# Two gated feed-forwards of layer 2 moved into the last steps of the rotary attention's loop, with silu written by tanh

## The chip, the core and the metric

The kernel runs as one program on one core of a Trainium2 chip. The metric is device time in microseconds for one execution of the whole program, the median of several executions. A profile of one further execution gives the trace that is read below. Engines are named as in the profile: PE is TensorE (matrix multiply), PEld its weight loads, DVE is VectorE, ACT is ScalarE, POOL is GpSimd, SP issues most DMAs.

## What is computed

Four layers act on one residual `x` of shape 4 x 1024 x 128 (batch, sequence, channels), all float32. Every layer is a "macaron": half a feed-forward, an attention, half a feed-forward, each behind a layer norm without gain. The reference, cut to the end of layer 1 and the start of layer 2 as the kernel numbers its stages (the reference calls the first of these modules L1):

```python
def _L1_ffn_ref(x, w_gate, w_up, w_down):        # DIM 128, HIDDEN 384, weights int / 127
    gate = jnp.einsum('bsd,hd->bsh', x, wg)
    up = jnp.einsum('bsd,hd->bsh', x, wu)
    h = jax.nn.silu(gate) * up
    return jnp.einsum('bsh,dh->bsd', h, wd)
...
x = x + 0.5 * _L1_ffn_ref(_layernorm(x, axis=-1), L1_ffn_w_gate, L1_ffn_w_up, L1_ffn_w_down)
x = x + _L1_attn_ref(_layernorm(x, axis=-1), L1_attn_w_qkv, L1_attn_w_out, L1_attn_b_out)
x = x + 0.5 * _L1_ffn_ref(_layernorm(x, axis=-1), L1_ffn_w_gate, L1_ffn_w_up, L1_ffn_w_down)
x = x + 0.5 * _L2_ffn_ref(_layernorm(x, axis=-1), L2_ffn_router_w, ...)    # mixture of experts, top 2 of 8
x = x + _L2_attn_ref(...)                                                   # linear attention with decay
```

`_L1_attn_ref` is a rotary softmax attention with 16 heads of 8 channels over 1024 positions. The third line, the gated feed-forward after the attention, is what the change is about: it stands between the rotary attention and the experts of the next layer, and each of the four batches has one of its own.

## The kernel before

**Stages.** `run` (L1284) goes through four stages in order: `l0`, `l1_attn`, `l2`, `l3`. The residual lies in SBUF for the whole run, one tile `X[b]` of 128 channels x 1024 positions for each batch. The stage `l1_attn` is the rotary attention. The stage `l2` begins with the gated feed-forward that follows it in the reference and then does the experts and the linear attention.

**The rotary attention, `l1_attn` (L629).** The work is cut into 256 units: 4 batches x 4 groups of four heads x 16 units, each unit one 128-wide slice against 512 positions. One loop (L800 to L826) with step `k` runs a pipeline. In step `k`, for each of two pairs of heads, it issues
- `greatest` (L713): two matmuls with 32 rows each into a PSUM tile `two` (128 x 1024, two banks), and a maximum over it on DVE (L720);
- `scores` (L735): two matmuls with 32 rows into PSUM tiles `s`, and the exponentials `e` on ACT (L743), for the unit `k - 11`;
- `values` (L745): matmuls of `e` with the values into the PSUM tile `o`, for the unit before that one.

Between steps, generators in the list `running` are advanced by one `yield` each (L826). They are the background steps: `shifted` (L722), `normalized` (L754), and `prepare` (L662), which for the next batch does the layer norm (project with the centring matrix `cen`, square it on ACT, sum it by eight 128 x 1 matmuls `var`, a square root on ACT, spread it by eight matmuls `bc`, and scale it on DVE to `xn`) and the projections with their rotation. `prepare` is started at `k % 64 == 10` for the next batch, so it runs three times inside the loop and not at all for the last 64 steps. From `k = 256` on there is no `greatest`, since only the second and third part of the pipeline are left; the loop ends with `k = 267`, and a last loop (L827) drains `running`.

**Order.** PE's order in this stage is the order of the program (`manual_schedule`, L641). The tiles `two` come from a pool with two buffers (L638), the tiles `s` from one with three, `o` has one; together they are all eight banks of PSUM. Every background step that uses PE takes one of the two `two` buffers and holds it until its last reader is done. The other engines are ordered by the scheduler of the framework, and each runs its own queue in order.

**Layer 2, `layer2` (L1255) and `l1_ffn` (L588).** `lanes` (L1188) interleaves generators by the costs that they yield. `first0` to `first3` are the gated feed-forwards of the batches (`l1_ffn`): layer norm of a batch, then in each half of 512 positions three pairs of matmuls `wg` and `wu` (128 x 128 with 128 x 512), `Silu` on ACT (L613), the product on DVE (L616), three matmuls `wd`, and `add_half` (L246), which adds half the result to `X`. `first0` and `first2` lie in one lane and `first1` and `first3` in another, so 0 and 1 run first. `route` for batches 0 and 1 (L276) waits for `first0` and `first1`; it computes the gating and the lists of tokens by which `experts` (L424) gathers its rows. No expert starts before a route is done.

Of the kernel before, what the change touches and what calls it, by code (L numbers as in the profile page):

```python
# [12 lines left out]
AF = mybir.ActivationFunctionType  # L13
ALU = mybir.AluOpType
AX = mybir.AxisListType

P = 128
# [4 lines left out]
HALF = 512  # L22
# [6 lines left out]
HIDC = 3  # L29
# [176 lines left out]
class Macaron:  # L206
# [36 lines left out]
            parts[part] = v  # L243
        return parts

    def add_half(self, b, c, o):  # L246

        X = self.X[b]
        self.nc.vector.scalar_tensor_tensor(X[:, c], o, 0.5, X[:, c], ALU.mult, ALU.add)

# [225 lines left out]
    def combine(self, ps, wp, batches, b, plan):  # L476

        nc = self.nc
        gt = len(batches) * NT
        n = batches.index(b)  # L480
        if n == 0:
            yield 9
        y = []
        for c in range(2):
            y.append(self.t(wp, [P, NT, D], f"c_y{c}", bufs=1))
            r = slice(c * gt * P + n * S, c * gt * P + (n + 1) * S)
            nc.sync.dma_start(out=y[c], in_=plan["res"][r, :].rearrange("(i p) d -> p i d", p=P))
        for h in range(2):
            tp = self.t(ps, [P, 4, P], "bank")
            for j in range(4):  # L490
                i = 4 * h + j
                nc.scalar.mul(y[0][:, i, :], y[0][:, i, :], plan["p1"][:, n * NT + i, :])
                nc.vector.scalar_tensor_tensor(
                    y[1][:, i, :], y[1][:, i, :], plan["p2"][:, n * NT + i, :], y[0][:, i, :], ALU.mult, ALU.add
                )
                nc.tensor.transpose(tp[:, j, :], y[1][:, i, :], self.c0["ident"])
            self.add_half(b, slice(h * HALF, (h + 1) * HALF), tp.rearrange("p i t -> p (i t)"))
        yield 6


# [87 lines left out]
    def l1_ffn(self, ps, wp, m, b):  # L588
        nc, c0 = self.nc, self.c0
        X = self.X[b]  # L590
        bank = lambda shape=(P, HALF): self.t(ps, list(shape), "bank")
        halves = [slice(h * HALF, (h + 1) * HALF) for h in range(2)]
        sq, xc = self.t(wp, [P, S], "sq", bufs=1), self.t(wp, [P, S], "xc", bufs=1)
        for c in halves:
            cen = bank()
            self.mm(cen, c0["center"], X[:, c])
            nc.scalar.activation(sq[:, c], cen, AF.Square)
            nc.vector.tensor_copy(xc[:, c], cen)
        r = self.scales(ps, wp, sq, "f")
        yield 4  # L600
        for hf, c in enumerate(halves):
            bc = bank((P, 4, P))
            for j in range(4):
                i = 4 * hf + j
                self.mm(bc[:, j, :], r[:, i : i + 1].to_broadcast([P, P]), c0["ident"])
            xn = self.t(wp, [P, HALF], "xn")
            nc.vector.tensor_tensor(xn, xc[:, c], bc.rearrange("p i t -> p (i t)"), ALU.mult)
            h = self.t(wp, [P, HIDC, HALF], "h", bufs=1)
            for i in range(HIDC):
                g = bank()  # L610
                self.mm(g, m["wg"][:, i, :], xn)
# [9 lines left out]
            self.add_half(b, c, o)  # L621
            yield 3


# [1 line left out]

    def l1_attn(self, m, c1):  # L629
        nc = self.nc  # L630
        scale = HD ** -0.5
        LEAD, RING = 11, 4
        v = nc.vector
        PE = mybir.EngineType.PE
        with ExitStack() as ctx:
# [23 lines left out]
                    self.mm(o[:, h * HALF : (h + 1) * HALF], w, x[:, h * HALF : (h + 1) * HALF])  # L659
                return o  # L660

            def prepare(b):  # L662
                c, X = self.c0, self.X[b]
                cen = project(c["center"], X)
                sq = self.t(self.lnp, [P, S], "sq", bufs=1)
# [15 lines left out]
                    self.mm(bc[:, i * P : (i + 1) * P], r[:, i : i + 1].to_broadcast([P, P]), c["ident"])  # L681
                xn = self.t(self.lnp, [P, S], "xn")
                v.tensor_tensor(xn, xc, bc, ALU.mult)
                yield
                yield
                for w, wt, tag in ((m["wq"], m["wqt"], "qd"), (m["wk"], m["wkt"], "kd")):
                    t1 = self.t(wp, [P, S], "rot1", bufs=1)
                    v.tensor_tensor(t1, c1["cos"], project(w, xn), ALU.mult)
                    yield
                    t2 = self.t(wp, [P, S], "rot2", bufs=1)  # L690
                    v.tensor_tensor(t2, c1["sin"], project(wt, xn), ALU.mult)
                    out = dense[b, tag] = self.t(wp, [P, S], tag, bufs=1)
                    nc.gpsimd.tensor_tensor(out, t1, t2, ALU.add)
                    yield
# [59 lines left out]
            def normalized(chunk, o):  # L754
# [20 lines left out]
                if g4 == 3:  # L775
# [15 lines left out]
                    v.scalar_tensor_tensor(X[:, c], y, m["bo"], X[:, c], ALU.add, ALU.add)  # L791
                    yield

            for _ in prepare(0):
                pass
            for n in range(RING):
                spread(n)
            units = B * 4 * 16
            running, nms, qms, pending, o = [], {}, {}, None, None
            for k in range(units + LEAD + 1):  # L800
# [3 lines left out]
                    spread(k // 16 + RING - 1)  # L804
                if k % 64 == 10 and k // 64 + 1 < B:
                    running.append(prepare(k // 64 + 1))
                if first is not None and first % 8 == 0:
                    nms[first // 8] = self.t(wp, [P, 4, 2, 4], "nm", bufs=3)
                    qms[first // 8] = self.t(wp, [P, HALF], "qm", bufs=3)
# [378 lines left out]
    def lanes(self, *lanes):  # L1188
        lanes = [list(lane) for lane in lanes]
        clock, active, done = [0.0] * len(lanes), [None] * len(lanes), set()  # L1190
        while any(lanes) or any(active):
            ready = []
            for n, lane in enumerate(lanes):
                if active[n] is None and lane and done.issuperset(lane[0][1]):
                    name, _, start = lane.pop(0)
                    active[n] = (name, start())
# [58 lines left out]
    def layer2(self, moe, m, right, enter, ffn):  # L1255
# [11 lines left out]
            yield 0  # L1267

        def more(route):
            first = lambda b: (f"first{b}", (), ffn(pf[b % 2], (side, main)[b % 2] if b < 2 else side, b))  # L1270
            attn = lambda b: (f"middle{b}", (f"combine0{b}", "swap"), lambda: self.l2_attn(side, pa[b % 2], m, decay, b))
            return (
                [first(0), first(2), attn(0), attn(2)],
# [9 lines left out]

    def run(self, stages):  # L1284
        nc = self.nc
        self.X = []
        self.c0 = self.load("c0")
        for b in range(B):
            X = self.t(self.res, [P, S], f"x{b}")
# [20 lines left out]
        for n, name in enumerate(stages):  # L1310
# [61 lines left out]
```

## Time and profile before

| what | value |
|---|---|
| runs | 3285.68, 3293.57, 3298.78 us (median 3293.57) |
| the profiled execution | 3296.3 us, span of its profile 3294.4 us |
| busy: PE / PEld | 2875.3 us (87%) / 1685.8 us (51%) |
| busy: DVE / ACT / POOL | 1826.5 us (55%) / 1649.2 us (50%) / 807.0 us (24%) |
| last `values` matmul of the rotary attention ends | 2035.13 us |
| first matmul of batch 2's feed-forward starts | 2081.07 us |
| first matmul with an expert's weights starts | 2159.66 us |
| mean granted clock of PE | 0.905 |

The page of the profile has six parts; the second shows the span in 40 slices of 82.4 us, with each engine's busy share in tenths. The rotary attention fills slices 11 to 24, layer 2 begins in slice 24. A timeline lists instructions by start and duration, with the idle time before them in brackets and what ended it. A table by stretches gives each engine's busy time between two times, and PE's granted clock there. A matmul in float32 shows as two records of PE.

### The profile page before, as it was taken

The page shows a single profiled execution, that of the slowest core. Times are in us where ns is not written, and L with a number is a line of the kernel's source. Part 1 is how long each engine was busy: PE and PEld are TensorE (multiplying, and loading weights), DVE is VectorE, ACT ScalarE, POOL GpSimd, SP SyncE. Part 2 cuts the span into 40 slices and gives each one's busy share as a digit, 9 for nine tenths or more (in the row PEclk, how much of TensorE's full clock was granted, in tenths as well). Part 3 has the DMA queues.
Part 4 walks back from the last instruction along what each step waited for, and adds up shares of the span by engine and source line. Part 5 has one row for each costly group of instructions (what it writes and reads, how often), then busy time and mean ns, then how long its engine had stood idle before and what let it go on. Part 6 is the DMA issues. An engine that isn't in the chain of part 4 may idle for free.

```text
span 3294.4 us, 48535 instructions
## 1 busy us (share of the span) xinstructions
PE 2875.3 (87%) x18206; PEld 1685.8 (51%) x18206; DVE 1826.5 (55%) x3160; ACT 1649.2 (50%) x3640; POOL 807.0 (24%) x748
## 2 busy tenths in 40 slices
PE   6888637878879999999999999988988977899997
PEld 6766426766643333333333333586777865344333
DVE  3376877774226676676776772431555521355664
ACT  3565524658613565566566565444444534444442
POOL 2565405552340000000000000046434454011110
PEclk7989858889977999999999999979989988788997
DMA  4766414663500000000000000157565666000000
GB/s 151 227 186 188 140 42 130 185 188 115 168 9 7 4 6 4 6 6 4 21 5 6 1 1 9 42 152 245 171 185 147 199 197 194 0 0 0 7 7 13
DMA packets 122890, 277.64 MB, mean 84 GB/s; under 512 B 18016, under 2 KB 67296, under 8 KB 122528
## 3 DMA queue, kind: packets, MB, share of 16 engines
q1 hardware_dynamic: 101792, 231.77, 23.8%
q0 software_dynamic: 20864, 42.77, 4.3%
q8 instruction: 144, 2.36, 0.3%
q14 instruction: 90, 0.74, 0.1%
HBM read 238.43 MB, written 31.85 MB: 82 GB/s over the span
## 4 chain that ended last, share of the span: by engine, by line
PE 74%; DVE 12%; ACT 5%; issue 4%; DMA 3%; POOL 1%; another core or an unknown queue 0%; SPq 0%; ACTq 0%; DVEq 0%; POOLq 0%
PE bank L227 40%; PE two L227 17%; PE o L227 8%; PE s L227 4%; DVE nm L720 2%; ACT e_h L468 2%; PE wave L1010 1%; DVE prod L545 1%; PE bank L461 1%; DMA c_y<-res 1%; DVE sc L530 1%; ACT L468 1%; DMA e_w<-in_l0m_dram 1%; DVE prod L528 1%; DVE e_x L463 1%
## 5 line engine op out<-in xcount | busy, mean ns | idle before, releaser
L720 DVE TENSOR_REDUCE nm<-two 128x2 f32<-128x1024 f32 x512 | 626.9, 1225 | 288.3 <-PE s L227 268.9
L743 ACT ACTIVATE e<-s 128x512 f32<-128x512 f32 x1024 | 556.4, 595 | 405.6 <-PE s L227 402.6
L468 ACT ACTIVATE e_h<-bank,e_w 128x128 f32<-128x128 f32 x1304 | 454.8, 368 | 511.6 <-PE bank L227 388.4
L227 PE MATMUL bank<-e_x,e_w 128*128 128x128 f32 x2608 | 569.3, 318 | 154.5 <-ACT e_h L468 79.9
L227 PE MATMUL s<-qm,kz 32*128 32x512 f32 x2048 | 634.1, 643 | 0.8 <-ACT e L743 0.8
L227 PE MATMUL two<-kz,qz 32*128 32x512 f32 x2048 | 593.2, 664 | 21.3 <-DVE nm L720 2.5
L227 PEld LDWEIGHTS bank<-e_x,e_w 128*128 128x128 f32 x2608 | 413.9, 204 | 291.3 <-ACT e_h L468 144.4
L457 POOL DMA_INDIRECT e_xg<-rows,g_source x326 | 334.4, 1026 | 835.1 <-DVE g_target L412 354.2
L227 PE MATMUL bank<-e_w,e_h 128*128 128x128 f32 x2608 | 445.7, 291 | 12.3 <-ACT e_h L468 6.9
L442 POOL DMA_INDIRECT res<-e_y,g_target x326 | 373.5, 1146 | 337.0 <-DVE e_y L441 152.7
L227 PEld LDWEIGHTS bank<-e_w,e_h 128*128 128x128 f32 x2608 | 378.8, 205 | 23.0 <-ACT e_h L468 13.3
L227 PE MATMUL o<-e,va 128*32 128x256 f32 x4096 | 328.8, 392 | 0.1
L441 DVE TENSOR_TENSOR e_y<-bank,e_w 128x128 f32<-128x128 f32 x326 | 94.3, 290 | 403.7 <-PE bank L227 317.0
L227 PEld LDWEIGHTS two<-kz,qz 32*128 32x128 f32 x2048 | 159.7, 189 | 239.9 <-issue 164.0
L227 PEld LDWEIGHTS o<-e,va 128*32 128x32 f32 x4096 | 81.0, 108 | 390.3 <-issue 370.3
L227 PEld LDWEIGHTS s<-qm,kz 32*128 32x128 f32 x2048 | 206.9, 183 | 10.9 <-issue 7.7
L708 POOL COPY va<-vd 128x256 f32<-128x256 f32 x16 | 6.7, 433 | 626.3 <-PE o L227 538.0
L1115 POOL TENSOR_TENSOR z<-st,r 128x512 f32<-128x512 f32 x32 | 46.2, 1445 | 417.1 <-DVE st L1108 333.7
L463 DVE COPY e_x<-bank 128x128 f32<-128x128 f32 x326 | 93.0, 285 | 92.2 <-PE bank L461 67.6
L227 PE MATMUL bank<-g_cols,g_lanes 128*128 128x39 f32 (+1 forms) x512 | 90.5, 341 | 28.9 <-DVE g_cols L392 28.8
L461 PE MATMUL bank<-c,e_xg 128*128 128x128 f32 x326 | 95.0, 291 | 21.7 <-DMA e_xg<-rows,g_source 21.6
L227 PEld LDWEIGHTS bank<-g_cols,g_lanes 128*128 128x128 f32 x512 | 91.2, 270 | 32.5 <-issue 31.4
(300 smaller groups left out, 3694.0 us busy)
## 6 DMA issues: line engine op xcount, KB each, us to landing
e_w<-in_l0m_dram SPq DMA_DIRECT2D x170, 578.0 KB
e_w<-in_l2m_dram SPq DMA_DIRECT2D x156, 578.0 KB
c_y<-res SPq DMA_DIRECT2D x32, 512.0 KB
rows<-g_xt SPq DMA_DIRECT2D x16, 512.0 KB
e_xg<-rows,g_source POOLq DMA_INDIRECT x326
res<-e_y,g_target POOLq DMA_INDIRECT x326
x<-in_x_dram SPq DMA_DIRECT2D x4, 512.0 KB
qz<-qd SPq DMA_DIRECT2D x64, 32.0 KB
```

Source lines behind the costliest of these rows:

```text
L227: self.nc.tensor.matmul(out, lhsT, rhs, start=start, stop=stop)
L441: nc.vector.tensor_tensor(y, o, w[:, MOE_W - D :], ALU.add)
L442: ins = nc.gpsimd.indirect_dma_start(out=res[:, :], out_offset=at(target[:, k : k + 1]), in_=y, in_offset=None)
L457: nc.gpsimd.indirect_dma_start(out=xg, out_offset=None, in_=rows[:, :], in_offset=at(source[:, k : k + 1]))
L461: nc.tensor.transpose(tp, xg, self.c0["ident"])
L463: nc.vector.tensor_copy(x, tp)
L468: nc.scalar.activation(h[:, fc, :], up[:, fc, :], func, bias=w[:, 2 * FC * P + fc : 2 * FC * P + fc + 1])
L528: v.tensor_tensor(pr, q.unsqueeze(2).to_broadcast(sh), k.unsqueeze(1).to_broadcast(sh), ALU.mult)
L530: v.tensor_reduce(sc, pr, AX.X, ALU.add)
L720: v.tensor_reduce(nm[:, it, h, 2 * pair : 2 * pair + 2], s, AX.X, ALU.max, negate=True)
L743: nc.scalar.activation(es[g], s, AF.Exp, scale=scale)
L1115: (pool if i else v).tensor_tensor(z, st[:, 0:HALF], r, ALU.mult)
```

## The change

`prepare` is split: its layer norm becomes `normal(b, out)`, which `prepare` calls and the new `feed` calls too. `feed(b, w)` does the gated feed-forward of batch `b` as background steps: the six yields of the layer norm, then for each half three steps with `wg` and `wu` into one `two` tile, an empty step, and one step with the three `wd` matmuls into a `two` tile and the addition to `X`. `feeds()` does this for batches 0 and 1 one after the other, and is put into `running` at `k = 240`, when both batches have left the attention. Its 32 steps reach beyond the loop's end at `k = 267`, so the last four run in the drain. `AF.Silu` is replaced by `tanh(gate / 2)` on ACT, `(tanh + 1) * gate` and the product with `up` on DVE, and a factor 0.25 in place of 0.5. The intermediate tiles use the buffers `rot1` and `rot2` of the last rotation. In `layer2`, `first0` and `first1` become empty tasks that are done at once. The feed-forwards of batches 2 and 3 stay where they are, with `Silu`.

```diff
+    def add_part(self, b, c, o, part=0.5):
-        self.nc.vector.scalar_tensor_tensor(X[:, c], o, 0.5, X[:, c], ALU.mult, ALU.add)
+        self.nc.vector.scalar_tensor_tensor(X[:, c], o, part, X[:, c], ALU.mult, ALU.add)
...
-            def prepare(b):
+            def normal(b, out):
                 c, X = self.c0, self.X[b]
                 cen = project(c["center"], X)
...
+                out.append(xn)
                 yield
                 yield
+
+            def prepare(b):
+                held = []
+                yield from normal(b, held)
+                (xn,) = held
...
+            def feed(b, w):
+                held = []
+                yield from normal(b, held)
+                (xn,) = held
+                for hf in range(2):
+                    c = slice(hf * HALF, (hf + 1) * HALF)
+                    h01, h2 = (self.t(wp, [P, 2, HALF], tag, bufs=1) for tag in ("rot1", "rot2"))
+                    hs, act = [h01[:, 0], h01[:, 1], h2[:, 0]], h2[:, 1]
+                    for i in range(HIDC):
+                        gu = two((P, 2, HALF))
+                        self.mm(gu[:, 0], w["wg"][:, i, :], xn[:, c])
+                        self.mm(gu[:, 1], w["wu"][:, i, :], xn[:, c])
+                        nc.scalar.activation(act, gu[:, 0], AF.Tanh, scale=0.5)
+                        v.scalar_tensor_tensor(act, act, 1.0, gu[:, 0], ALU.add, ALU.mult)
+                        v.tensor_tensor(hs[i], act, gu[:, 1], ALU.mult)
+                        yield
+                    yield
+                    o = two((P, HALF))
+                    for i in range(HIDC):
+                        self.mm(o, w["wd"][:, i, :], hs[i], start=i == 0, stop=i == HIDC - 1)
+                    self.add_part(b, c, o, 0.25)
+                    yield
+
+            def feeds():
+                for b in fed:
+                    yield from feed(b, fed[b])
...
+                if k == units - 16:
+                    running.append(feeds())
...
-            first = lambda b: (f"first{b}", (), ffn(pf[b % 2], (side, main)[b % 2] if b < 2 else side, b))
+            first = lambda b: (f"first{b}", (), ffn(pf[b % 2], (side, main)[b % 2] if b < 2 else side, b) if b not in self.fed else tuple)
...
-                    self.l1_attn(weights("l1a"), weights("c1"))
+                    self.fed = {b: weights("l1f") for b in range(2)} if "l2" in stages else {}
+                    self.l1_attn(weights("l1a"), weights("c1"), self.fed)
```

More of the change, by code (lines that the diff above doesn't have):

```diff
@@ L244, in load @@
         return parts
-    def add_half(self, b, c, o):
+    def add_part(self, b, c, o, part=0.5):
         X = self.X[b]
-        self.nc.vector.scalar_tensor_tensor(X[:, c], o, 0.5, X[:, c], ALU.mult, ALU.add)
+        self.nc.vector.scalar_tensor_tensor(X[:, c], o, part, X[:, c], ALU.mult, ALU.add)
     def centered(self, w, n):
@@ L496, in combine @@
                 nc.tensor.transpose(tp[:, j, :], y[1][:, i, :], self.c0["ident"])
-            self.add_half(b, slice(h * HALF, (h + 1) * HALF), tp.rearrange("p i t -> p (i t)"))
+            self.add_part(b, slice(h * HALF, (h + 1) * HALF), tp.rearrange("p i t -> p (i t)"))
         yield 6
@@ L620, in l1_ffn, with l1_attn @@
                 self.mm(o, m["wd"][:, i, :], h[:, i, :], start=i == 0, stop=i == HIDC - 1)
-            self.add_half(b, c, o)
+            self.add_part(b, c, o)
             yield 3
-    def l1_attn(self, m, c1):
+    def l1_attn(self, m, c1, fed):
         nc = self.nc
@@ L1195, in lanes @@
                     name, _, start = lane.pop(0)
-                    active[n] = (name, start())
+                    active[n] = (name, iter(start()))
                     clock[n] = max(clock[n], min([clock[o] for o in range(len(lanes)) if o != n and active[o]] or [0]))
@@ L1285, in run @@
         nc = self.nc
-        self.X = []
+        self.X, self.fed = [], {}
         self.c0 = self.load("c0")
```

## Prediction, made before the changed kernel ran

> **What bounds the kernel now.** I read the slices of the page first, then a table by stretches around the change, then timelines inside them.
>
> ```profile
> PE   6888637878879999999999999988988977899997
> PEclk7989858889977999999999999979989988788997
> ```
>
> Slices 11 to 24 are the rotary attention and the start of layer 2. PE is at nine tenths or more throughout, with its clock whole except for short stretches.
>
> ```profile
> 1935.12:1993.60 58.48, 57.95 (x525) 20.05 (x524) 41.69 (x40) 35.72 (x66) 0.00 (x0) 1.00 0.00 1
> 1993.60:2035.13 41.53, 41.44 (x293) 13.60 (x290) 2.14 (x5) 24.96 (x46) 0.00 (x0) 1.00 0.01 1
> 2035.13:2081.07 45.94, 44.96 (x158) 24.11 (x159) 17.90 (x31) 13.91 (x23) 0.00 (x0) 1.00 0.05 15
> 2081.07:2138.30 57.23, 55.84 (x245) 35.23 (x243) 30.74 (x73) 31.90 (x85) 0.00 (x0) 0.97 0.18 60
> 2138.30:2162.20 23.90, 23.87 (x108) 22.94 (x108) 5.49 (x17) 8.83 (x36) 6.20 (x7) 0.50 0.13 37
> ```
>
> The columns are the stretch, its length, then busy time of PE, PEld, DVE, ACT and POOL, then the clock. Row 1 is where the first moved feed-forward goes (`greatest` still runs), row 2 where most of the second goes (no `greatest`), row 3 is where both stand now, row 4 the feed-forwards of batches 2 and 3 with the first routing, row 5 the end of that routing. PE is busy for 99% of rows 1 and 2 and 98% of row 3. So the work leaves a stretch that PE bounds and enters one that PE bounds; what counts is whether a matmul costs more PE time at the new place than at the old.
>
> Row 2 could mislead: without `greatest`, only pairs of `s` with 32 rows are left, so half of the array's rows seem free.
>
> ```profile
> 2024.93 0.64 PE L227 MATMUL o<-e,va 128*32 128x256 f32 x8
> 2025.50 1.13 PE L227 MATMUL two<-heads,attn_w 128*128 128x512 f32 x2
> 2026.56 1.13 PE L227 MATMUL s<-qm,kz 32*128 32x512 f32 x4
> ```
>
> Here one full matmul (`wo`) stands between a pair's `o` and the next `s`: `s` starts 1.06 us after it. It lies beside nothing. TensorE: Matmul & The Clock Gate, "Part 3: Packing small matmuls — row/col tiling", says that matmuls run at the same time when they use different row groups; a 128-row matmul uses all. By a reading in which the idle rows take it, the second feed-forward would be nearly free; by the row it is paid in full.
>
> **The change part by part.** The two listings of PE's instructions hold the same matmuls, 159 of them at other places; POOL's and SP's queues, DMAs included, are in the same order. So no DMA is added or passed.
>
> *What leaves layer 2.* The last `o` ends at 2035.13 and batch 2's feed-forward starts at 2081.07: 45.9 us. In the changed listing PE has there, besides work of batch 2 and of the routing, three pairs `wg`, `wu` and one group of three `wd`, which are the rest of the second feed-forward, and what stood there before: the transposes of `os` and `on` (0.49 and 0.44 from start to start), `wo` (0.96), and two small matmuls (0.63). At full stream a 512-column matmul takes 0.86:
>
> ```profile
> 2067.34 1.02 PE L227 MATMUL bank<-xn,l1f_wg 128*128 128x512 f32 x2
> 2068.20 1.02 PE L227 MATMUL bank<-xn,l1f_wu 128*128 128x512 f32 x2
> 2069.06 1.02 PE L227 MATMUL bank<-xn,l1f_wg 128*128 128x512 f32 x2
> ```
>
> Nine of them make 7.7, with 2.5 for the others 10.2. **Saved: 45.9 - 10.2 = 35.7 us.** The chain of the last pair (tanh, two DVE operations, `wd`) may show by up to 2.5 us; work of batch 2 and of the routing stands in PE's queue between, so I take 0.
>
> *What enters the loop.* `prepare` already does the same kind of step at the same place, so its rows price `feed`. I take the time from one unit's first exponential to the next, 3.49 us for a plain unit.
>
> ```profile
> 1273.98 1.09 ACT L743 ACTIVATE e<-s 128x512 f32<-128x512 f32 x2 [0.70 <-PE s L227]
> 1276.26 1.98 PE L227 MATMUL two<-x,c 128*128 128x512 f32 x4
> 1280.09 1.11 ACT L743 ACTIVATE e<-s 128x512 f32<-128x512 f32 x2
> 1280.26 0.70 PE L227 MATMUL two<-kz,qz 32*128 32x512 f32 x2 [0.38 <-ACT xc L668]
> 1316.31 1.98 PE L227 MATMUL two<-xn,attn_w 128*128 128x512 f32 x4
> 1318.22 0.70 PE L227 MATMUL two<-kz,qz 32*128 32x512 f32 x2
> ```
>
> - Centring (`cen`): 1280.09 - 1273.98 = 6.11, so +2.62: 1.91 of matmul, the rest waits behind the two ACT passes over 1024 columns. Twice: 5.2.
> - Sums and square root (`var`): in the last `prepare` its unit goes from 1543.64 to 1550.33, 6.69, against 4.28 for a unit with the same transposes: +2.41. Twice: 4.8.
> - Spread (`bc`): 1296.36 to 1303.01 is 6.65 against 4.15 for a unit with transposes: +2.50. Twice: 5.0.
> - A pair `wg`, `wu`: like a projection, 1318.22 - 1316.31 = 1.91. Nine of the twelve are before the last `o`: 17.2.
> - Three `wd`: 1.06 + 2 x 0.86 = 2.78 (one matmul alone as in the `wo` rows, two more at full stream). Three groups before the last `o`: 8.3.
> - Transposes and a `two` tile of `feed` in one step, twice while `greatest` runs: a projection in such a unit costs 7.52 - 5.46 = 2.06, so +0.15 each: 0.3.
>
> **Added: 40.8 us.** DVE's two operations per pair (128 x 512 from PSUM, 0.69 each by L616 and L249) fit: with two maxima of 1.225 a unit has 3.83 us of DVE in 5.40. ACT gets 0.60 more in a unit with 2.2 of exponentials. Queued behind the tanh are exponentials, behind the two DVE operations maxima; both are waited for by PE through the ring of three `s` and two `two`.
>
> *The wait that is added.* A gate-up tile is held from its first matmul for 1.06 (to the start of ACT, as from 2067.34 to L613 at 2068.40) + 0.60 + 2 x 0.69 + two handovers of 0.06 = 3.2 us. The second `greatest` after it wants that buffer 1.91 + 1.64 = 3.55 us after that start. That is a margin of 0.35, so I take 0; if a maximum of 1.22 goes in between on DVE, each of the six pairs under `greatest` loses 0.9, together 5.3. The listing has the two operations ahead of those maxima.
>
> *Tanh.* No trace row has tanh between exponentials of this loop, but layer 3 has the sequence:
>
> ```profile
> 2852.78 0.59 ACT L1033 ACTIVATE t<-bank 32x512 f32<-32x512 f32 x1 [0.32 <-PE bank L227]
> 2853.83 0.69 ACT L1066 ACTIVATE wdec<-bank,attn_w 128x512 f32<-128x512 f32 x1 [0.47 <-PE bank L227]
> ```
>
> L1033 is tanh, L1066 exp, and no table load (1.28 where there is one) stands between: 0. The square root's two loads are inside the `var` price.
>
> *Clock.* After the first normalisation at whole clock the granted clock was halved for 6.8 us from 1288.3, just after PE had waited 0.77 for the square root; `var` and the unit after it then cost 3.36 + 1.64 = 5.0 instead of 2.41. After the last `prepare` it was not. I take it once in the two: **+2.6**. The same page, "Part 1: The HAM clock gate (the "warmup" mystery)", lets the clock fall after an idle window of about 3.4 us. No wait here is that long, so by the rule nothing falls and the sum would be 2.6 lower; the row at 1288 fell all the same, and I keep it.
>
> **Sum: 40.8 + 2.6 - 35.7 = +7.7 us.** On the profiled execution's 3296.3 that is 3304.0; on the median of the runs, 3293.57, it is 3301.3. I predict 3301. A measurement of this kernel tells about 0.5% (16.5 us) from no change, so this counts as no change. What is late next: after the saved stretch, batch 2's feed-forward, the routing and the experts have the same matmuls in nearly the same order, so they move as a block.
>
> Bounds: every matmul at its streaming pace with no stall makes the loop's part 34.0 (18 of `wg`, `wu` and 9 of `wd` at 0.86, and 2 x 5.4 for the normalisations' 1.72 + 1.84 + 1.85): net -1.7. With clock loss in both (+2.6 more), the lost margin (+5.3) and the drain's chain (+2.5) it is +18.
>
> **The rivals.**
> - *The routing's half-clock stretch goes* (row 5, 23.9 us at 0.50, worth 12.0 us). For: layer 2 opens with less dense matmul ahead of it. Against: the same small matmuls (128 x 39, 128 x 8) fill it. Net -4: 3289.
> - *Idle rows take the feed-forward* (row 2): its 16 us in the loop cost nothing. Against: the `wo` rows. Net -8: 3285. With the stretch above, and bare pace elsewhere, -24: 3270, faster.
> - *The clock falls in the attention's end* (slower): full-array matmuls, 128 x 1 sums and waits mixed may bring a long half-clock stretch where now there is none for 792 us (1295.2 to 2087.1). One as long as row 5 costs 12.0, so net +20: 3313; it decides once more than 18 us at half clock are added beyond the 6.8.
> - *It does not do what it says*: a table is reloaded at each tanh, 24 loads x 1.28 = up to 31 us of ACT, by `var`'s case (2.41 for 1.80 of matmul) at least 0.6 a pair: net +15 to +38, middle 3320. Against: the layer 3 rows, and the listing has no load there.
>
> **How the numbers follow.** Forecast 0.55; stretch gone alone 0.11; idle rows alone 0.04; the combination, faster by over 0.5% (below 3277), 0.09; clock falls 0.18, of which 0.02 stays below 3310; reload 0.03. So faster 0.09, within 0.5% 0.55 + 0.11 + 0.04 + 0.02 = 0.72, slower 0.16 + 0.03 = 0.19. The range goes from 3286 (the stretch gone, and the runs' own spread) to 3318 (the clock case): left out are the combination, the reload and the far end of the clock case, some 0.2.
>
> **What would show it.** In the changed profile the loop's units with a pair should take 5.4, with `cen` 6.1, the loop should end 43 us later (last `o` near 2078), and batch 2's first matmul should start some 10 us after it. Right or wrong apart: units with a pair over 6 (the buffers), half clock between 1935 and 2080 (the clock), units in the tail at 3.4 with a pair in them (idle rows), table loads in the loop beyond four. The forecast is wrong if the experts' first matmul does not simply move by about 8 us from 2159.66.

## The result, and the profile after

| | changed kernel | kernel before |
|---|---|---|
| median of 20 runs | 3291.42 us | 3286.76 us |
| lowest to highest | 3273.26 to 3304.80 | 3277.78 to 3302.42 |
| ratio, 95% interval | 1.0004, 0.9987 to 1.0020 | |
| profiled execution, span | 3281.62 us, 3279.4 us | 3296.30 us, 3294.4 us |

No measurable difference, as forecast in kind (0.72 on that). In size the forecast of 3301 us, a ratio of 1.0023, lies just outside the interval. The means differ by 1.2 us (a ratio of 1.0004), the medians by 4.7. The 20 runs spread by 1%, and go with the mean granted clock (correlation -0.78): the longest span, 3302.6 us, had 0.902, and 3275.1 us had 0.914.

The slices of the changed kernel:

```profile
PE   6888637878879999999999999988988976899997
PEclk7889857889877999999999998999998989888997
```

PE's busy share in slices 13 to 28 reads as before. The clock does not: slice 25, the loop's end, has 8 where it had 9, and slice 27, the routing, has 9 where it had 7. Next the table by stretches of the changed kernel (stretch, length, busy time of PE, PEld, DVE, ACT, POOL, then the clock). The rows are the loop from unit 240 to 256 and from there to the last `o`, the rest of the second feed-forward, batch 2's feed-forward with the routing, and the routing's end up to the experts' first matmul.

```profile
1926.95:2014.37 87.42, 81.97 (x601) 30.10 (x604) 52.12 (x56) 43.94 (x78) 0.00 (x0) 0.98 0.00 1
2014.37:2076.35 61.98, 61.98 (x345) 24.32 (x345) 7.96 (x13) 31.30 (x54) 0.00 (x0) 0.86 0.00 1
2076.35:2086.60 10.25, 10.25 (x45) 6.18 (x44) 5.06 (x10) 4.21 (x8) 0.00 (x0) 1.00 0.00 0
2086.60:2132.80 46.20, 44.79 (x188) 26.87 (x189) 23.41 (x62) 30.36 (x75) 0.00 (x0) 1.00 0.12 37
2132.80:2156.70 23.90, 23.56 (x141) 19.34 (x140) 13.36 (x31) 9.88 (x40) 4.10 (x5) 0.87 0.38 130
```

Row 2 is the surprise: PE is busy for all of 61.98 us and the clock is 0.86 all the same. Row 5 had 0.50 before and has 0.87 now. Below, **loop** is from unit 240's first exponential to the last `o`, **opening** from there to the experts' first matmul, and "at whole clock" is a time less half of what it spent at half clock, bracketed in the table. That is an estimate: the kernel broad, further down, shows that a microsecond at half clock cost the loop 0.39 us, not 0.5.

| profile | loop | opening | both | both at whole clock |
|---|---|---|---|---|
| before, three executions | 99.97, 99.95, 99.95 (0) | 124.57 (24.8), 120.96 (16.8), 120.99 (16.8) | 222.1 (mean) | 212.1, 212.5, 212.5 |
| changed, three executions | 149.40, 149.97, 149.43 (20.5 each) | 80.35 (6.1), 80.37 (6.2), 80.41 (6.3) | 230.0 (mean) | 216.4, 217.0, 216.5 |

By this estimate the loop grew by 39.2, 39.8 and 39.2 us (predicted 40.8; 41.4 by broad) and the opening shrank by 34.9, 35.3 and 35.3 (predicted 35.7). With the clock as it came, the stretch is 7.85 us longer (predicted 7.7). The whole kernel is not.

Two timelines of the changed kernel show the steps. First a pair `wg`, `wu` under the maxima:

```profile
1960.22 1.13 PE L227 MATMUL two<-xn,l1f_wg 128*128 128x512 f32 x2
1961.18 1.02 PE L227 MATMUL two<-xn,l1f_wu 128*128 128x512 f32 x2
1962.13 0.70 PE L227 MATMUL two<-kz,qz 32*128 32x512 f32 x2
1962.30 0.60 ACT L813 ACTIVATE rot<-two 128x512 f32<-128x512 f32 x1 [1.50 <-PE two L227]
1963.35 1.08 ACT L749 ACTIVATE e<-s 128x512 f32<-128x512 f32 x2 [0.45 <-PE s L227]
1963.65 0.69 DVE L815 TENSOR_TENSOR rot<-rot,two 128x512 f32<-128x512 f32 x1
1964.39 0.70 PE L227 MATMUL two<-kz,qz 32*128 32x512 f32 x2 [0.55 <-DVE rot L815]
```

The pair costs 1962.13 - 1960.22 = 1.91 as priced; the tanh (L813) stands before an exponential with no table load between. The last line is the wait that the prediction put at a margin of 0.35: PE stands 0.55 until L815 has freed the buffer. Next, the second normalisation in the tail:

```profile
2023.82 0.64 PE L227 MATMUL o<-e,va 128*32 128x256 f32 x8
2024.38 1.30 PE L227 MATMUL s<-qm,kz 32*128 32x512 f32 x4
2025.62 0.64 PE L227 MATMUL o<-e,va 128*32 128x256 f32 x8
2026.19 2.24 PE L227 MATMUL two<-c,sq 128*128 128x1 f32 x16
2028.36 2.08 PE L227 MATMUL s<-qm,kz 32*128 32x512 f32 x4
2030.36 1.08 PE L227 MATMUL o<-e,va 128*32 128x256 f32 x8
2031.37 2.08 PE L227 MATMUL s<-qm,kz 32*128 32x512 f32 x4
...
2040.43 3.78 PE L227 MATMUL two<-c,rstd 128*128 128x128 f32 x16
2044.01 0.97 PE L769 MATMUL two<-c,os 128*128 128x128 f32 x4
2044.90 1.13 PE L227 MATMUL s<-qm,kz 32*128 32x512 f32 x4
```

The clock falls at 2027.7, during the eight 128 x 1 sums, and for 17.1 us everything takes longer (`s` 2.08 instead of 1.13, `o` 1.08 instead of 0.64); PE never waits.

### The profile page after: what moved, and what is told of

It is laid out like the page before. It is cut to its first block, busy times and chain, and to the rows that moved or that the text cites. A ratio compares the mean times of both kernels' runs of the same rounds, so it can differ in the third digit from the quotient of the medians.

```text
span 3279.4 us, 48534 instructions
## 1 busy us (share of the span) xinstructions
PE 2860.9 (87%) x18206; PEld 1667.5 (51%) x18206; DVE 1830.7 (56%) x3166; ACT 1652.7 (50%) x3644; POOL 801.9 (24%) x748
## 4 chain that ended last, share of the span: by engine, by line
PE 74%; DVE 12%; ACT 5%; issue 4%; DMA 3%; POOL 1%; SPq 0%; another core or an unknown queue 0%; DVEq 0%; ACTq 0%; POOLq 0%
PE bank L227 39%; PE two L227 18%; PE o L227 8%; PE s L227 4%; DVE nm L726 2%; ACT e_h L468 2%; PE wave L1046 1%; DMA c_y<-res 1%; DVE prod L545 1%; PE bank L461 1%; DVE sc L530 1%; ACT L468 1%; DVE st L1144 1%; DVE e_x L463 1%; PE acc L1046 1%
## 5 line engine op out<-in xcount | busy, mean ns | idle before, releaser
L227 PE MATMUL bank<-e_w,e_h 128*128 128x128 f32 x2608 | 444.9, 290 | 10.2 <-ACT e_h L468 6.3
L442 POOL DMA_INDIRECT res<-e_y,g_target x326 | 364.4, 1118 | 331.5 <-DVE e_y L441 143.4
L227 PE MATMUL bank<-g_cols,g_lanes 128*128 128x39 f32 (+1 forms) x512 | 82.2, 320 | 28.9 <-DVE g_cols L392 28.8
L227 PEld LDWEIGHTS bank<-g_cols,g_lanes 128*128 128x128 f32 x512 | 82.2, 247 | 32.1 <-issue 30.8
```

The source lines that it names most:

```text
L227: self.nc.tensor.matmul(out, lhsT, rhs, start=start, stop=stop)
L442: ins = nc.gpsimd.indirect_dma_start(out=res[:, :], out_offset=at(target[:, k : k + 1]), in_=y, in_offset=None)
```

## Experiments

The first theory is the prediction's sum, with the clock's places as a matter of two stretches that cancel. Its rivals: the experts give the difference back; the waits behind the square root make the clock fall; the one-column sums do. (The expectations letter their theories anew each time, so a letter does not mean the same in all of them.) The first eight experiments ran on two chips where the kernel before takes 3215.9 and 3215.5 us, the others on chips where it takes 3283 to 3290, so ratios are compared, not times.

### Both kernels again

again_before and before2 are the kernel before, again_after and after2 the changed one, each without an edit.

> The kernel before, unchanged, for a second profile. Stretch L runs from the first exponential of unit k = 240 to the first matmul with an expert's weights in layer 2; it was 224.5 us with 24.8 us at half clock (all in layer 2's opening) before, and 229.8 us with 26.6 us at half clock (20.5 in the loop, 6.1 in the opening) in the changed kernel. With half of the half-clock time taken off it is 212.1 and 216.4. Theory A (the move itself costs 4 to 5 us; half-clock stretches fall where they fall): 211 to 213 again after that subtraction, with another length of half clock. Theory C (the stretch of 24 us at half clock at the end of the first routing belongs to this kernel): 22 to 26 us at half clock there again. Theory B (the changed kernel gains in the experts' part by its slightly other order): 620 us again from the first to the last expert matmul.

> The changed kernel, unchanged, for a second profile and a narrower interval. Theory A: the loop's part (first exponential of k = 240 to the last o) less half of its half-clock time 138 to 140 us again, the opening less half of its half-clock time 76 to 78; L so corrected 215 to 218; ratio 1.000 to 1.003. Theory B: 612 us for the experts' part again, against 620 before, and a ratio at or under 1.000. Theory C: half clock 17 to 21 us in the loop's end again, 6 in the opening.

> The changed kernel once more, with five rounds, for the size of its ratio and for a third profile. Forecast of the record: ratio 1.0023. The two measurements so far give 1.0004 and 1.001. By the stretch from unit 240 to the experts' first matmul, which was 5.2 and 9.4 us longer in two pairs of profiles, it should be 1.0016 to 1.003; in the profile 13.7 to 20.5 us at half clock in the loop and 6 to 7 us at half clock in the opening, as in the two before.

> The kernel before once more, for a third profile: ratio 1.000 with at most 0.002 on either side; no half clock from unit 240 to the last o, 17 to 24 us at half clock in the opening, and 220 to 225 us from unit 240 to the experts' first matmul. If the half-clock stretch in the opening is absent or in the loop here, the clock's places are chance and not the change's.

Before: 1.0003 (0.9989 to 1.0018) and 0.9996 (0.9975 to 1.0016). Changed: 1.0010 (0.9999 to 1.0022) and 1.0010 (0.9989 to 1.0031); the last interval holds the forecast 1.0023, the other two of the changed kernel end just below it, and the 1.0016 to 1.003 that was expected of after2 was missed. The half-clock stretches of the loop came at the same units in all three profiles of the changed kernel (3.4 to 6.8 us after unit 242, 13.7 to 17.1 at units 258 to 260), and in none of the three before. The experts' part at whole clock is 581.8, 547.0, 581.6 us before and 583.0, 546.9, 583.4 changed (the middle one on the faster chip): the experts give nothing back.

The means of the changed kernel's runs lie 1.2, 3.2 and 4.9 us above those of the kernel before on the same chip, each with an uncertainty of 3 to 5 us; weighted together that is 3.2, give or take 2.2. Over 273 runs of all the kernels here, each taken against the mean of its own kernel and chip, a mean clock higher by 0.001 goes with a time 1.5 us shorter (correlation -0.72). In the last two comparisons the mean clock was higher with the change, by 0.0009 and 0.0005, which is not clear of its own scatter and would be worth -1.3 and -0.7 us.

### The two halves of the change

skip leaves the moved feed-forwards out altogether (two of the four after the attention are missing); double does them in both places, so applies them twice.

```diff
# skip
-                if k == units - 16:
-                    running.append(feeds())
# double
-  ffn(...) if b not in self.fed else tuple)
+  ffn(...))
```

> Only layer 2's part of the change: first0 and first1 are empty and no feed runs in the loop, so the feed-forwards of batches 0 and 1 are left out of the computation. By the sum that was on record, the work in layer 2's opening is 45.9 - 2.5 = 43.4 us at whole clock, so the time falls by 43 us, to about 3246 (ratio 0.987), under theory A give or take 6 of clock; the loop's end as in the kernel before (100 us from k = 240 to the last o). If the opening hid part of that work beside something else, it falls by less.

> Only the loop's part: feeds run in the loop and layer 2 does first0 and first1 again, so these two feed-forwards are applied twice. By the sum on record the loop's part costs 40.8 up to the last o and 7.7 for the rest in the drain at whole clock, 48.5; theory A: plus 48 us, some 3337 (ratio 1.0147), plus or minus 8 of clock. If the loop had room for the work (idle rows of the array beside the pairs of s), clearly less than 40.

skip: 0.9863 (0.9837 to 0.9889), -44 us. double: 1.0159 (1.0140 to 1.0178), +51 us. Their sum, +7, is the change's local price. The saving is real and so is the cost: -43 and +48 were expected of matmuls that are paid in full, so nothing is hidden in idle rows of the array, and nothing was off the path.

### Where the feeds begin

```diff
-                if k == units - 16:
+                if k == units - 96:     # early
+                if k == units - 26:     # mid
```

> Feeds start at k = 160 instead of 240, so both feed-forwards end under greatest and none of their steps is left for the loop's end or the drain. From the first exponential of k = 160 to the last o the kernel before takes 398.6 us, the changed one 448.0 and 448.6, each with 20.5 us of half clock, of which 17.1 and 13.7 lie behind the square root of the second feed, where greatest no longer runs. Theory A (half clock falls anywhere): 398.6 + 40.8 + 8.5 for the three pairs and one wd that now come before the last o, and 1 or 2 for two-buffer collisions, 449 to 450 at whole clock, half clock between 0 and 20. Theory C (the long stretch belongs to the place without greatest): at most 7 us of half clock behind each square root, so 450 to 456; the opening as when the loop has no feeds in its end, 83 to 84 with 24 to 28 us of half clock.

> The changed kernel, but the feeds begin at unit 230 instead of 240: both normalisations now lie under the maxima (centrings at units 230 and 246), and only the second feed-forward's pairs and down projections lie in the tail. If the fall of the clock in the tail comes from the second normalisation's place there, no half-clock stretch of over 6.8 us is left between units 240 and the last o, as in the kernel whose feeds began at unit 160; time from unit 224's first exponential to the last o at whole clock about as in the changed kernel, plus up to 4 us for two-buffer collisions of a few more pairs. If the rest of the second feed-forward in the tail is enough for it, 13.7 us or more at half clock stay there. In the opening the routing's half-clock stretch is expected to come back to 17 to 24 us if it goes by what lies in the tail shortly before, and to stay at 6.8 if it goes by the pairs. By the price of the loop and the opening at whole clock (+5 to +8) the ratio to before is 1.001 to 1.004 either way.

early: 1.0055 (1.0035 to 1.0076). Its loop's end is that of before (99.94 us, no half clock), and its 32 units with feeds had none either, but took some 55 us more instead of 49: more pairs meet the maxima with two buffers (from unit 160 to the last `o` 453.2 us, where 449 to 450 was expected). The opening has a 23.9 us half-clock stretch again. mid: 1.0026 (1.0004 to 1.0048). In the tail the half clock is gone, 3.4 us are left at unit 232. From unit 224 to the experts' first matmul it takes 281.5 us at whole clock against 275.5 for the changed kernel, so the collisions cost 4 to 6 us (4 with the half clock priced as in broad), where up to 4 was expected. The opening has 13.1 us at half clock, which fits neither of the two values expected. The clock in the tail follows the place of the second normalisation; moving it costs at least as much as it brings.

### Silu in the loop, and the order in layer 2

```diff
# silu
-  nc.scalar.activation(act, gu[:, 0], AF.Tanh, scale=0.5)
-  v.scalar_tensor_tensor(act, act, 1.0, gu[:, 0], ALU.add, ALU.mult)
+  nc.scalar.activation(act, gu[:, 0], AF.Silu)
# defer
-  (f"first{b}", (), ffn(...
+  (f"first{b}", () if b < 2 else ("route00",), ffn(...
```

> The feeds in the loop with Silu on ACT and one product on DVE in place of tanh and two DVE operations. Each of the twelve pairs then brings two table loads of 1.28 us among the exponentials. By the case of the square root (0.6 of wait for two loads) at least 7 us more than the changed kernel, at most 31 us when nothing hides them: loop's end 157 to 180 us instead of 149.4 and 150.0, ratio to before 1.003 to 1.011. If the loads are hidden behind PE: no more than 2 us.

> The changed kernel with first2 and first3 started only when the first route's program is through, so that the scheduler puts half of their matmuls behind the first experts. Theory E (layer 2's opening is bound by PE, the experts' part has idle PE): first expert 15 to 22 us earlier after the last o (opening 58 to 65 instead of 80.4), experts' part longer by less, ratio to before 0.994 to 0.999. Rival (the experts' part is bound by PE as well, or loses what it is given): experts' part longer by 15 to 22, ratio 1.000 to 1.003.

silu: 1.0037 (1.0017 to 1.0057); the loop takes 145.3 us at whole clock against 139.2 to 139.8. ACT has 22 table loads in the loop instead of 4; the 18 more, at 1.28 us each, cost 5 to 6 us of the 23 that they last. The loop's 152.1 us, with 13.7 at half clock, lie below the 157 to 180 that were expected. So tanh is worth 5 to 6 us here. defer: 1.0032 (1.0017 to 1.0047). The experts start sooner (opening 62.9 instead of 77.3 at whole clock) and take 562.3 instead of 546.9: what is pulled out of the opening is paid among the experts, which PE bounds too.

### What makes the clock fall in the tail

noroot leaves the square root out of the two moved normalisations. wide leaves out sums, root, reciprocal and spreading, and scales by two 512-column matmuls with the matrix of means. thinonly puts the one-column sums back, read by a DVE copy alone; spreadonly has the spreading matmuls, of a constant, and no sums.

```diff
# noroot
-  nc.scalar.activation(std, var, AF.Sqrt, bias=self.eps_ln)
-  v.reciprocal(r, std)
+  v.reciprocal(r, var)
# wide, in place of var, std, r and bc
+  bc = project(c["mean"], sq)
+  v.tensor_tensor(xn, xc, bc, ALU.mult)
# thinonly: as wide, and at the place of the sums
+  for i in range(NT):
+      self.mm(var[:, i : i + 1], sq[:, i * P : (i + 1) * P], c["mean"][:, 0:1])
+  v.tensor_copy(r, var)
# spreadonly: as wide, but bc by
+  for i in range(NT):
+      self.mm(bc[:, i * P : (i + 1) * P], c["mean"][:, 0:1].to_broadcast([P, P]), c["ident"])
```

> The square root is left out in the layer norm of the two feeds (x is divided by the variance), and with it its two table loads, four in all, and the wait of PE for them; the 128 x 1 matmuls stay. Theory D (the clock falls in the loop because PE waits there for ACT): no half clock in the loop, sums at 1.9 to 2.0 each, the loop's end 136 to 138 us instead of 149.4 and 150.0, and the whole kernel 10 to 12 us under the changed one, ratio to before 0.997 to 0.998. Rival (the thin 128 x 1 matmuls themselves let it fall): half clock 13 to 21 us in the loop as it was, loop 146 to 149.

> The changed kernel, but in the two feeds' normalisations alone the eight sums of one column each, the square root, the reciprocal and the eight spreading matmuls are replaced by two matmuls of 512 columns with the constant matrix of means, which sum and spread at once; xn is multiplied by that tile. So root and reciprocal are left out of these two normalisations. The centring stays at units 240 and 256, the spreading at 244 and 260, and the pairs where they were. Theory 1 (the clock falls in the tail because of the thin matmuls of 128x1 that stand between waits there): no half clock between units 256 and 264, against 13.7 to 17.1 us at units 258 to 260 in the four kernels with a second normalisation there; loop some 139 us whatever else, of which 4 to 5 us less for the two sums (2.4 each), so about 135, and the ratio to before about 1.000. Theory 2 (it falls because of the waits for ACT behind the centring, or because full-array matmuls mix with 32-row ones): 13.7 us or more at half clock stay between units 256 and 264, loop about 142. Theory 3 (the clock answers to what ran long before, some tens of us): the half-clock stretch comes, but at another unit than 258 to 260.

> As the kernel with wide sums, and the eight sums of one column each are put back at units 242 and 258, into a tile that only a DVE copy of 8 columns reads; root, reciprocal and the spreading matmuls stay out, and xn is again the centred tile times the wide sums. If the narrow sums by themselves make the clock fall in the tail, a half-clock stretch of 13.7 us or more begins within 6 us of unit 258's first exponential. If it takes the spreading matmuls of 128x128 or the wait for the reciprocal, there is none, as with the wide sums alone, and the loop takes about 141 us.

> As the kernel with wide sums, but with the eight spreading matmuls of 128x128 at units 244 and 260 and no sums at all: the spread values are the constant 1/128, so the two normalisations leave out the sums, root and reciprocal. If the narrow sums make the clock fall, there is no half clock between units 256 and 266 here and the loop takes about 137 us. If the spreading matmuls do, a stretch of 6.8 us or more begins within 6 us of unit 260's first exponential.

noroot: 1.0021 (1.0006 to 1.0035), loop 146.64 us with 13.7 at half clock in the tail: the wait for the square root is not the whole cause. wide: 0.9973 (0.9952 to 0.9994), loop 136.60 us, no half clock. thinonly (one run): 3.4 us after the first sums, 13.7 us after the second. spreadonly (one run): loop 136.74, none. The table by stretches of thinonly (before the sums, the sums, after them):

```profile
2022.66:2026.09 3.43, 3.43 (x29) 1.09 (x25) 0.00 (x0) 1.83 (x5) 0.00 (x0) 1.00 0.00 0
2026.09:2027.96 1.87, 1.87 (x20) 1.86 (x16) 0.00 (x0) 0.50 (x2) 0.00 (x0) 1.00 0.04 9
2027.96:2041.60 13.64, 13.64 (x51) 3.47 (x51) 0.17 (x1) 4.83 (x9) 0.00 (x0) 0.51 0.00 1
```

PE is busy in all of it, no engine holds it up, and the clock halves 0.2 us after the end of 1.87 us of one-column matmuls. So it is the narrow sums.

real_tail leaves nothing out: its second normalisation has wide sums and takes root and reciprocal over 1024 columns.

```diff
+  var = project(c["mean"], sq)
+  nc.scalar.activation(sq, var, AF.Sqrt, bias=self.eps_ln)
+  v.reciprocal(sq, sq)
```

> The changed kernel, complete, but the second feed's normalisation alone (in the tail, without maxima) sums and spreads in one step by two matmuls of 512 columns with the matrix of means, takes the square root over 1024 columns on ACT and the reciprocal over 1024 columns on DVE, whose 128-column reciprocal takes 0.95 us elsewhere, so 7.6 us by that row, inside the four units from the sums to the first pair. If the narrow sums make the clock fall, the tail has no half clock, the loop takes some 136 to 140 us instead of 149.4 to 150, and from unit 240 to the experts' first matmul some 217 to 220 us against 229.8 for the changed kernel and 221 to 224.5 for the one before: ratio to before 0.997 to 1.000. If the fall has another cause, 13.7 us of half clock stay and the ratio is 1.000 to 1.002. If the reciprocal is too slow for the four units, PE waits at unit 262.

real_tail: 1.0035 (1.0018 to 1.0052). This is above the ranges that either theory gave (up to 1.002). No one-column sums in the tail, yet 23.9 us at half clock, from another cause. PE's timeline of it:

```profile
2032.18 0.64 PE L227 MATMUL o<-e,va 128*32 128x256 f32 x8
2032.75 1.12 PE L227 MATMUL s<-qm,kz 32*128 32x512 f32 x2
2035.92 2.07 PE L227 MATMUL s<-qm,kz 32*128 32x512 f32 x2 [2.05 <-ACT e L761]
```

Two table loads and a root over 1024 columns hold the exponentials up; PE waits 2.05 us, and at the end of that the clock is half. So some 2 us of either, a wait or one-column matmuls, can do it. Neither always does: over all the traces here, 142 of 214 waits of 2.0 to 2.5 us that began at whole clock had a fall in them or within 1.5 us after.

### The sums made wide

broad takes each sum in the two moved normalisations with 128 columns and reads column 0. broad_all does so in the other normalisations too (64 columns in the feed-forwards), broad_before in the kernel before. They leave nothing out.

```diff
-  var = two((P, NT))
...
-  self.mm(var[:, i : i + 1], sq[...], c["mean"][:, 0:1])
+  var = two((P, NT, P))
...
+  self.mm(var[:, i, :], sq[...], c["mean"])
+  var = var[:, :, 0]
```

> The changed kernel, complete, with one edit in the two feeds' normalisations: each of the eight sums takes 128 columns of the matrix of means instead of one, and column 0 is read on. The wait for the square root stays as it is. The eight spreading matmuls of the same shape cost 2.50 us a unit, the narrow sums 2.41, so some 0.2 us more at whole clock. If the clock falls because the sums are one column wide, the tail has no half clock or no more than 3.4 us, from unit 240 to the experts' first matmul it is 218 to 222 us against 229.8, and the ratio to before is 0.997 to 0.999. If eight matmuls of 128x128 with the wait behind them are enough, 13.7 us at half clock stay and the ratio is 1.000 to 1.003.

> As the kernel before it, and the sums of the rotary attention's own normalisations, of the feed-forwards (64 columns), of the l2 attention and of layer 3's time block are as wide. If narrow sums make the clock fall elsewhere too, the total at half clock goes below the 600 us of the changed kernel by some 20 to 60 us, worth 10 to 30 us of time: ratio 0.988 to 0.996. If the fall is the tail's alone, the ratio is as for the kernel before it.

> The kernel before the change with the same wide sums throughout. It tells whether the moved feed-forwards pay once the narrow sums are gone: by the price at whole clock the change costs 5.1 us less what the opening's half clock gives, so broad_all against this one is +0 to +5 us. Ratio to before 0.990 to 0.998, or 1.000 if narrow sums do nothing elsewhere.

The loop of broad, by stretches (units 240 to 256, and from there to the last `o`), and PE at the second normalisation's sums:

```profile
1927.62:2014.20 86.58, 81.12 (x601) 30.09 (x604) 52.16 (x56) 44.14 (x78) 0.00 (x0) 1.00 0.00 1
2014.20:2069.24 55.04, 55.04 (x345) 21.54 (x345) 7.96 (x13) 31.50 (x54) 0.00 (x0) 1.00 0.00 1
...
2026.01 2.05 PE L227 MATMUL two<-c,sq 128*128 128x128 f32 x16
2028.00 1.13 PE L227 MATMUL s<-qm,kz 32*128 32x512 f32 x4
```

The same numbers of matmuls as in the changed kernel, 55.04 us instead of 61.98 in the tail, clock whole, though the square root and its two table loads still stand among the exponentials. So it is the width. The other traces agree: half clock begins during or within 2.5 us after 75 of the 93 groups of one-column sums in the rotary attention of all twenty profiles, and after none of the 12 groups with 128 columns.

broad also measures the loop with the clock whole: 141.62 us. Its wider sums cost 0.11 us more each time (unit 258 takes 5.94 us, and 5.83 in silu, where the clock is whole there too), so with narrow sums it would be 141.4, which is 41.4 above the kernel before. The 20.5 us at half clock in the changed kernel then cost 149.4 - 141.4 = 8.0 us.

From unit 240 to the experts' first matmul broad takes 223.2 us (218 to 222 was expected) against 230.0 for the changed kernel and 222.1 for the one before. The whole kernel has 1.0020 (0.9997 to 1.0043), where 0.997 to 0.999 was expected; the 1 us that the stretch is longer than before, 1.0003, lies inside. Its profile has 603 us at half clock against 600, 542 and 603 for the changed kernel. The clock's slices of broad_before:

```profile
PEclk9888857889987999999999999989998989889887
```

broad_before: 0.9963 (0.9946 to 0.9980), -12 us, the one complete version here that beats both kernels. Its clock is 0.9165 against 0.9082 (means over runs); at 1.5 us for 0.001 that is the whole 12 us. Its profile has 550 us at half clock, broad_all's 495. broad_all: 1.0001 (0.9978 to 1.0023), clock 0.9145, where 0.988 to 0.996 was expected. Its mean is 9.3 us above that of broad_before, give or take 6.6, where 0 to 5 was expected; the medians' ratio is 1.0036 (0.9998 to 1.0052). The change does not pay there either.

## Why the prediction was right or wrong

- **Saved 35.7:** right, 34.9 to 35.3. The last `o` ended at 2076.35 (near 2078 was said), batch 2's feed-forward began 10 us after it.
- **Added 40.8:** right as a sum, 41.4 by broad. `cen` +2.62 at unit 240 (predicted 2.62), but +2.06 in the tail, where no maxima wait. Pairs 1.91, `wd` 2.77: as priced. The collisions were put at 0.3 and are larger: units 247, 248 and 252 take 5.81, 7.04 and 7.51 us, 0.41, 0.86 and 1.32 more than a pair explains, together 2.6. The margin of 0.35 was not there. The tail gave 2.2 back: `cen` +2.06, the spreading +1.82 instead of 2.50 (unit 260 of broad), the last `wd` +2.16 instead of 2.78, and small ones.
- **Tanh 0:** right; four table loads in the loop, the square roots' own.
- **Idle rows, reload:** did not occur.
- **Clock +2.6: the step that failed.** "I take it once in the two: +2.6" was drawn from one dip of 6.8 us in the kernel before, which the prediction put "just after PE had waited 0.77 for the square root". Its lines, with the clock of the stretch from the wait's start:

```profile
1285.87 1.95 PE L227 MATMUL two<-c,sq 128*128 128x1 f32 x16
1287.67 0.63 PE L763 MATMUL two<-c,os 128*128 128x128 f32 x4
1289.08 1.22 PE L227 MATMUL two<-kz,qz 32*128 32x512 f32 x2 [0.77 <-DVE rstd L676]
1288.30:1295.10 6.80, 6.03 (x33) 1.47 (x32) 2.75 (x5) 2.97 (x5) 0.00 (x0) 0.50 0.00 0
```

  The wait runs from 1288.31 to 1289.08, and the clock is at half from its start, half a microsecond after the one-column sums. The same trace has a dip of 3.4 us at 1032.3, behind the sums of the `prepare` before, which the prediction did not count. What the runs showed in place of the 2.6: the loop got 20.5 us at half clock in each of three profiles, 8.0 to 8.6 us of time, behind the narrow sums: the rival "the clock falls in the attention's end". At the same time the opening's half clock went from 16.8 to 24.8 us down to 6.2, 5 to 9 us of time by halving: the rival "the routing's half-clock stretch goes". The two were priced as alternatives and came together. In the stretch they net to +1.6; that the local sum came out at 7.85, near 7.7, is therefore partly luck. The whole execution did not follow it: +3.2, give or take 2.2. The difference of 4 to 5 us lies outside the stretch. There the clock is the likely place (602 us at half clock on average in the three profiles before: 627, 572, 607; 582 in the three after: 600, 542, 603), but with such a scatter it is not shown whether the change does that or chance.
- **"They move as a block":** half right. The experts at whole clock are unchanged, but the experts' first matmul moved by -3 us, not +8, because the part before unit 240, with the same instructions, was 8.2 us shorter in that execution. Half clock in that part ranges from 338 to 372 us over the four profiles of the two kernels on the slower chips. So here a sum of one stretch did not carry over to the whole below some 10 us.

The prediction weighed the rule of the Trainium skill in TensorE: Matmul & The Clock Gate, "Part 1: The HAM clock gate (the "warmup" mystery)", that the clock falls after an idle window of about 3.4 us. The runs agree that half clock comes in steps of that length (3.4, 6.8, 10.2, 13.7, 17.1, 23.9 us). They differ on the cause: 2.05 us of waiting was enough in real_tail, and in thinonly 1.87 us of one-column matmuls with PE busy all the time.

**What stays open.** Why the routing's half clock in the opening shrinks: it is 6.1 to 6.3 us after the change, 5.9 with wide, 9.4 with broad, 20.7 with thinonly, 27.5 with early, and no edit here isolates it. Why the same narrow sums cost 13.7 to 17.1 us of half clock in the tail and at most 6.8 under the maxima. And why broad, 7 us shorter in the stretch than the changed kernel, isn't shorter as a whole; the half clock of other parts differs by more than that from run to run.

## What to carry to other kernels

Moving work between two stretches that the same engine bounds brought nothing here: price the matmuls at both places, and expect the difference to be waits for buffers. Where the forecast is a few microseconds, look at which narrow matmuls the move carries along: a group of one-column sums was followed by up to 17.1 us at half clock. Summing into 64 or 128 columns instead of one made the kernel before 0.4% faster, though each sum is no shorter. And before a dip of the clock is put on a wait, compare when each of the two begins.

## What was not expected of the hardware

- A busy PE at half clock: 17.1 us at 0.50, begun within a group of eight 128 x 1 matmuls (16 records, 2.24 us); with 128 x 128 in their place (2.05 us) none.
- The same sums under the maxima were followed by 3.4 to 6.8 us of half clock or none, in the tail by 13.7 to 17.1.
- The spread of the runs goes with the clock: 1.5 us for 0.001 of mean clock over 273 runs, correlation -0.72.
